# A masked attention layer and an edge-score layer in one hand-ordered kernel: two block transposes are moved to later steps, odd heads use the second score bank in the first nine slots, and the tail gets a second place for sums

## The chip, the cores and the metric

The kernel runs on one core of a Trainium2 chip. The metric is the device time of one launch in microseconds (us). Before the change it was 3078.11 us, the median of three runs (3077.22 to 3081.56).

## The reference

The input is `x`, 16 graphs of 1024 nodes with 256 features in float32, and `adj`, 16 matrices of 1024 x 1024 in int32, which hold only 0 and 1 here.

```python
# layer 0: masked attention, 8 heads of 32
h = relu(layernorm(x))
Q, K, V = (heads(h @ W.T + b) for W, b in ((Wq, bq), (Wk, bk), (Wv, bv)))
s = where(adj == 0, -inf, Q @ K.T * 32 ** -0.5)
x = x + merge_heads(softmax(s) @ V) @ Wo.T + bo
# layer 1: edge scores of one kind of edge
h = relu(layernorm(x))
e = leaky_relu((h * a_0) @ h.T, 0.2)
x = x + softmax(where(adj == 1, e, -9e15)) @ h
```

The reference has weights `a_1` to `a_3` for entries of 2 to 4 in `adj` as well. The kernel counts such entries and has a branch for them at its end, which is not entered with these inputs.

## The kernel before

**Tiles and slots.** A graph has 8 tiles of 128 rows, so there are 128 tiles in all. Tile `t` of graph `b` is worked on in slot `s = 8 b + t`. A slot has eight steps, one for each head `h` of the tile that is in work (`now`, class `Attend`). The order of all instructions is written out by hand under `tc.manual_schedule()`: each engine runs its own instructions in exactly the order in which the loop names them, and waits where its data is not there. Beside `now`, a slot carries on five other things:

- `was`, the tile of the slot before. Its heads 6 and 7 are turned in steps 0 and 1. Then come `reciprocals` (step 1, L506 and L507 on VectorE), their turn on TensorE (step 2, L515), the copy `recT` on ScalarE (step 3, L519), `combine(1)` (heads 4 to 7, step 3, L525), `combined` (L535), `output` (step 4, L540), and `residual` (step 5, L546).
- `gone`, the tile before that: its normed rows are written for layer 1 and turned.
- `edge`, a tile of layer 1 that runs `LAG` = 9 slots behind (class `Edges`): two halves of scores in steps 0 and 2, `softmax_max` in step 3 (L654), `bend`, `leak`, and the exponential in step 6. Its scores go to `sides[1]`.
- `edge_was`, layer 1's tile of the slot before: its matrix of weights `sel` is turned in step 0, gathered against the node features in steps 5 and 6 (L696), and stored (L705).
- `piece`, 128 rows of the next graph, whose queries, keys and values are projected (L267, L344).

**A head's way.** `scores(h)` (L460) makes 128 x 1024 scores on TensorE in a PSUM place of two banks. There are two such places: `sides[0]`, and `sides[1]` for heads 4 and 6 and for layer 1. `softmax_max(h)` (L472, "max(h)" below) on VectorE adds the mask, writes `p` and gives the negated row maximum `nmx`; it also frees the place. One step later `softmax_exp(h)` (L489, "exp(h)") runs on ScalarE, and two steps after the scores the head is turned so that its columns lie on the partitions. After heads 0 to 3 are turned, `combine(0)` multiplies them with the values in step 7 (L525).

**Two ways to turn.** Most heads are turned by eight TensorE transposes (L589), with copies out of PSUM (L590). Heads 0, 1, 4 and 5 (`MIXED`; only 0 and 1 in tiles with t = 7, only 4 and 5 in tiles with t = 0), and layer 1's matrix always, go "by blocks": `turn_blocks` transposes blocks of 32 x 32 on VectorE (L381), and `place_blocks` moves them with four DMAs of 128 KB to their place in `pT` (L386). All these DMAs are issued by SyncE (SP), in the written order with its other DMAs: the queries of the next tile (`load_queries`, L427, 512 KB, step 3), the keys of the next graph (in slots with t = 7 and t = 0), `keep` and the output. Loads of `adj` and `x` and the writes of projected queries (`qd`) and keys (`kd`) are issued by GpSimd (POOL).

**The order around the change.** In step `h` of the loop the written order is: scores(h), max(h), exp(h-1), then in step 3 `recT`, `combine(1)` and `combined`, then the turn of head h-2 (so head 1 is turned in step 3, head 2 in step 4), then the parts that belong to fixed steps, among them:

```python
if h == 0:
    ...
    if edge_was:
        edge_was.turn_blocks()
        edge_was.place_blocks()
if h == 1:
    ...
    if was:
        was.reciprocals()
```

so on VectorE layer 1's block transpose lies between max(0) and max(1), and the reciprocals lie between max(1) and max(2). On SP head 1's four placing DMAs are issued before the queries of the next tile.

**The tail.** After slot 127 and a last part-slot for what is left over, nine tiles of layer 1 follow one another without a layer 0 beside them: tile 7 of graph 14, and the eight tiles of the last graph (`last`). Iteration i scores tile i, turns and places tile i-1, stores tile i-3, and gathers tile i-2. The last graph's scores alternate between the two sides, and odd tiles take other buffers for some of their data (`tags`). All gathers go to `sums_place`, the first half of one PSUM bank, which has also taken the sums of `combine`; its other half is `brief`. The second such bank has the halves `early` and `late`.

Of the kernel before, what the change touches and what calls it, by code (L numbers as in the profile page):

```python
# [8 lines left out]
F32 = mybir.dt.float32  # L9
# [5 lines left out]
ALU = mybir.AluOpType  # L15
AX = mybir.AxisListType

P = 128
HEADS = 8
HD = 32  # L20
# [10 lines left out]
def by_blocks(t):  # L31
    return BY_BLOCKS.get(t, MIXED)
# [7 lines left out]
FLOOR = 1e28  # L40
# [7 lines left out]
def gnn_kernel(  # L48
# [18 lines left out]
    nc = tc.nc  # L67
    B, N, D = x.shape
    NT = N // P
    NC = D // P  # L70
    SCALE = HD ** (-0.5)
    HALF = 512
    NB = P // HD
    LAG = NT + 1
# [9 lines left out]
    work = ctx.enter_context(tc.tile_pool(name="work", bufs=2))  # L84
# [10 lines left out]
    sums_place, brief, early, late = (banks[i // 2][:, i % 2, :] for i in range(4))  # L95


    sides = [ps_s.tile([P, N], F32, tag=f"s{i}", name=f"s{i}") for i in range(2)]
# [293 lines left out]
    h1s, x1ds, masks = {}, {}, {}  # L392
# [22 lines left out]
    class Attend:  # L415
# [3 lines left out]
        def __init__(self, b, t):  # L419
            self.b, self.t = b, t  # L420
            self.rows = slice(t * P, (t + 1) * P)
            self.probs, self.turned = {}, {}

        def load_queries(self):
            self.qt = work.tile([P, HEADS, P], F32R, tag="qt")
# [28 lines left out]
            )  # L454

        def scores(self, h):
            self.ps = sides[h in (4, 6)]
            for nh in range(N // HALF):
                cols = slice(nh * HALF, (nh + 1) * HALF)
                nc.tensor.matmul(  # L460
                    self.ps[:, cols],
                    lhsT=self.qt[:, h, :],
                    rhs=keysets[self.b][h][:, cols],
                    start=True,
                    stop=True,
                )

        def softmax_max(self, h):

            p = work.tile([P, N], F32, tag="p", bufs=4)  # L470
            nmx = small.tile([P, 1], F32, tag="nmx")
            nc.vector.tensor_tensor_reduce(  # L472
                out=p, in0=sides[h in (4, 6)], in1=self.neg, scale=-SCALE, scalar=FLOOR,
                op0=ALU.add, op1=ALU.min, accum_out=nmx,
            )
            self.probs[h] = (p, nmx)
# [116 lines left out]
    class Edges:  # L593


        def __init__(self, b, t, last=False):
            self.b, self.t, self.last = b, t, last
            self.rows = slice(t * P, (t + 1) * P)
            self.side = sides[t % 2 if last else 1]
            self.tags = {"sel": ("p", 4), "pT1": ("pT", 7)} if last else {}  # L600
            if last and t % 2:
                self.tags |= {"ha": ("hT", 1), "x1b": ("x1", 1)}

        def buffer(self, tag, shape):
            tag, bufs = self.tags.get(tag, (tag, 1))
# [86 lines left out]
        def gather(self, half):  # L692

            for j in range(half * NT // 2, (half + 1) * NT // 2):
                for a in range(NB):
                    nc.tensor.matmul(  # L696
                        sums_place[a * HD : (a + 1) * HD, :], lhsT=self.pT[:, j, a], rhs=h1s[self.b][:, j, :],
                        start=(j == 0), stop=(j == NT - 1),
                    )

        def store(self):
            rec = small.tile([P, 1], F32, tag="rec1")
            nc.vector.reciprocal(rec, self.total)  # L703
            ot = work.tile([P, D], F32, tag="h0", bufs=1)
            nc.vector.scalar_tensor_tensor(ot, sums_place, rec, self.x1, ALU.mult, ALU.add)  # L705
            nc.sync.dma_start(out=mixed(out[self.b, self.rows, :]), in_=ot)


# [76 lines left out]
    with tc.manual_schedule():  # L785
        first = [Piece(0, 0, 4), Piece(0, 4, 4)]
        piece_was, piece_next = Piece(1, 0), piece_of(0)
        now, nxt = attend_of(0), attend_of(1)
# [48 lines left out]
        for s in range(B * NT + 1):  # L837
# [9 lines left out]
            for h in range(HEADS):  # L847
                ending, eh = (now, h - 1) if h >= 1 else (was, HEADS - 1)
                turning, th = (now, h - 2) if h >= 2 else (was, HEADS + h - 2)

                load_keys(h, 0)


                if now:
                    now.scores(h)
                if h == 0 and piece_was:
                    piece_was.halve(0)
                if s == 0 and h == 1:
                    first[1].values()
                if h == 3 and edge:  # L860
                    edge.softmax_max()
                if h == 5:
                    if was:
                        was.residual()
                    norms(was, piece_nxt)
                if h == 6 and edge_was:
                    edge_was.gather(1)
                if now:
                    now.softmax_max(h)
                if h == 6 and edge_was:  # L870
                    edge_was.store()


                if h == 1 and edge:
                    edge.keep(0)
                if h == 2 and gone:
                    gone.turned_normed()
                if ending:
                    ending.softmax_exp(eh)

                if h == 3 and was:
                    was.turned_reciprocals()
                if h == 3 and edge:
                    edge.bend()
                    edge.keep(1)


                if h == 3:
                    if was:
                        was.combine(1)  # L890
                    if piece_was:
                        piece_was.biased()
                    if was:
                        was.combined()
                if turning and th in by_blocks(turning.t):
                    turning.turn_blocks(th)
                    turning.place_blocks(th)
                elif turning:
                    turning.turn(th, 0)
                    turning.turn(th, 1)  # L900


                if h == 0:
                    if edge:
                        edge.score(0)
                    if gone:
                        gone.normed()
                    if edge_was:
                        edge_was.turn_blocks()
                        edge_was.place_blocks()  # L910
                if h == 1:
                    if gone:
                        gone.turn_normed()
                    if piece_was:
                        piece_was.project(1, 0)
                        piece_was.project(1, 1)
                    if was:
                        was.reciprocals()
                    if piece_nxt:
                        piece_nxt.load()  # L920
                if h == 2:
                    if edge:
                        edge.score(1)
                    if piece_was:
                        piece_was.values()
                    if was:
                        was.turn_reciprocals()
                        was.add_bias()
                if h == 3:
                    if nxt:  # L930
                        nxt.load_queries()
                    if edge:
                        edge.leak()
                    if edge_was:
                        edge_was.load_nodes()
                    if nxt:
                        nxt.flag()
                        nxt.mask()
                if h == 4:
                    if was:  # L940
                        was.output()
                    if piece_was:
                        piece_was.raised(1)
                        piece_was.halve(1)
                    if piece:
                        piece.normed()
                    if piece_was:
                        piece_was.write_queries()
                    if edge_nxt:
                        edge_nxt.prepare()  # L950
                    if nxt2:
                        nxt2.load()
                if h == 5:
                    if edge_was:
                        edge_was.gather(0)
                    if piece:
                        piece.turn()
                    if piece:
                        piece.turned()
                if h == 6:  # L960
                    if edge:
                        edge.softmax_exp()
                    if was:
                        was.keep()
                    if now:
                        now.load_nodes()
                    if piece:
                        piece.project(0, 0)
                        piece.project(0, 1)
                if h == 7:  # L970
                    if now:
                        now.combine(0)
                    if piece:
                        piece.raised(0)
                load_keys(h, 1)
# [87 lines left out]
```

## Time and profile before

| what | value |
|---|---|
| median of three runs | 3078.11 us |
| profiled execution | 3080.43 us |
| its span, from the first instruction to the last | 3078.1 us |
| TensorE (PE) busy | 2964.1 us, 96% |
| ScalarE (ACT) busy | 2654.2 us, 86% |
| VectorE (DVE) busy | 2514.7 us, 82% |
| GpSimd (POOL) busy | 2172.2 us, 71% |
| slot 0 starts / slot 8 / slot 9 / slot 127 | 41.99 / 216.86 / 239.32 / 2970.17 us |
| length of a slot in the middle, by t from 0 to 7 | 24.4, 23.8, 23.0, 22.7, 22.5, 22.5, 22.1, 23.8 us |
| lengths of slots 1 to 4 | 19.9, 20.1, 21.7, 20.3 us |
| lengths of slots 121 to 126 | 22.4, 21.9, 21.6, 21.6, 21.5, 21.4 us |

A slot starts where scores(0) of its tile starts on PE. A line of a timeline gives the start in us, the length in us, the engine, the line of the kernel, the operation, its output and inputs, the shapes and a count of like instructions, and in square brackets the idle time of the engine just before it with what ended it. A line of the waits gives the instruction that waited, what it waited for, the total in us, how many times, and the longest. A line of the windows gives the stretch, its length, the busy time of PE, PE's weight loads, DVE, ACT and POOL (each with a count of instructions), the granted TensorE clock as a share of full speed, the busy share of the DMA engines and GB/s. A line of DMA issues ends with KB each and the median us from issue to landing.

### The profile page before, as it was taken

Reading aid. Unit: us, or ns where it says so; the run is one execution under the profiler, and the core shown is the slowest. Engines: PE = TensorE matmul, PEld = TensorE weight load, DVE = VectorE, ACT = ScalarE, POOL = GpSimd, SP = SyncE. Lnnn points to the kernel's source line nnn. Section 1 sums busy time; section 2 is a strip of 40 time slices with the busy share of each in tenths; the row PEclk is TensorE's granted clock in tenths of the full one; section 3 lists DMA queues with packets and bytes.
Section 4 is the critical chain, followed back from the end, with each engine's and each line's share of the span. In section 5 each row is a group of like instructions: output and inputs, shape, how many; then the busy total and the mean of one; then the engine's idle time right before and its main releaser. Section 6 shows DMA issues by size and latency. Waiting matters only on the chain. (4 is left out here: it accounts for less than half of the span.)

```text
span 3078.1 us, 96258 instructions
## 1 busy us (share of the span) xinstructions
PE 2964.1 (96%) x36722; PEld 2230.7 (72%) x36722; DVE 2514.7 (82%) x4453; ACT 2654.2 (86%) x5159; POOL 2172.2 (71%) x2999
## 2 busy tenths in 40 slices
PE   7889999999999999999999999999999999999997
PEld 4667777777777777777777777777777777776664
DVE  5878888888888888888888788888888888888884
ACT  5889888899888898889889888988989888898872
POOL 3657777777777777777777777777777777776542
PEclk9999999999999999999999999999999999999999
DMA  6776777878777786777777777787777777777653
GB/s 239 217 227 201 235 236 225 253 219 245 229 224 235 227 257 212 227 251 221 247 230 232 233 231 244 221 253 223 221 248 226 248 212 234 236 227 239 191 164 100
DMA packets 597828, 695.68 MB, mean 226 GB/s; under 512 B 63280, under 2 KB 528560, under 8 KB 597360
## 3 DMA queue, kind: packets, MB, share of 16 engines
q1 hardware_dynamic: 528288, 477.29, 52.0%
q0 software_dynamic: 66960, 210.04, 20.8%
q8 instruction: 295, 4.83, 0.7%
q10 hardware_dynamic: 2112, 2.10, 0.2%
q14 instruction: 173, 1.42, 0.1%
HBM read 252.98 MB, written 134.22 MB: 126 GB/s over the span
## 5 line engine op out<-in xcount | busy, mean ns | idle before, releaser
L472 DVE CUSTOM_DVE_ANT_0 p<-s,neg 128x1024 f32<-128x1024 f32 x1024 | 1235.6, 1207 | 220.8 <-PE s L460 189.5
L489 ACT ACTIVATE p<-p,nmx 128x1024 f32<-128x1024 f32 x1024 | 1249.6, 1224 | 135.5 <-DVE nmx L472 127.1
L460 PE MATMUL s<-k,qt 128*128 128x512 f32 x2048 | 759.3, 452 | 22.2 <-DVE nmx L472 13.8
L590 ACT COPY pT<-trp 128x512 f32<-128x512 f32 x1024 | 548.7, 590 | 92.8 <-PE trp L589 92.3
L589 PE MATMUL trp<-ident,p 128*128 128x128 f32 x4608 | 603.9, 274 | 3.6 <-ACT pT L590 1.5
L589 PEld LDWEIGHTS trp<-ident,p 128*128 128x128 f32 x4608 | 531.3, 140 | 101.7 <-DVE pT L590 9.6
L381 DVE STREAM_TRANSPOSE blocks<-p 128x1024 f32<-128x1024 f32 x456 | 564.4, 1238 | 12.7 <-ACT p L678 10.6
L525 PE MATMUL acc<-pT,v 128*32 128x128 f32 x16384 | 533.3, 275 | 36.9 <-ACT recT L519 24.9
L525 PEld LDWEIGHTS acc<-pT,v 128*32 128x32 f32 x16384 | 454.3, 110 | 146.3 <-ACT recT L519 79.9
L696 PE MATMUL acc<-h,pT 128*32 128x256 f32 x8192 | 493.0, 382 | 8.0 <-DVE ot L705 7.9
L440 POOL TENSOR_SCALAR neg<-adj 128x1024 bf16<-128x1024 int32 x128 | 467.7, 3654 | 43.7 <-ACT neg L452 34.4
L460 PEld LDWEIGHTS s<-k,qt 128*128 128x128 f32 x2048 | 322.0, 190 | 116.4 <-DVE nmx L472 43.7
L696 PEld LDWEIGHTS acc<-h,pT 128*32 128x32 f32 x8192 | 241.0, 109 | 210.3 <-issue 62.4
L674 POOL TENSOR_TENSOR sel<-sel,less 128x1024 f32<-128x1024 f32 x120 | 286.6, 2388 | 69.4 <-ACT less L663 48.1
L631 PE MATMUL s<-h1T,ha 128*128 128x512 f32 (+2 forms) x744 | 272.8, 490 | 2.6 <-ACT h1T L568 0.5
L672 POOL TENSOR_SCALAR less<-top 128x1 f32<-128x1 f32 x120 | 31.8, 265 | 272.9 <-DVE top L654 272.8
L324 POOL DMA_DIRECT2D qd<-halves x240 | 177.0, 777 | 58.7 <-POOL halves L314 31.8
L489 ACT ACTIVATION_READ_ACCUMULATOR p<-p,nmx 128x1 f32 x1024 | 206.8, 202 | 0.0
L509 POOL COPY wide<-rec 128x256 f32<-128x256 f32 x128 | 53.7, 419 | 208.9 <-DVE rec L507 208.9
L330 POOL DMA_DIRECT2D kd<-halves x240 | 171.7, 764 | 35.5 <-POOL halves L314 35.4
L314 POOL TENSOR_TENSOR halves<-full,halves 128x256 fp32r<-128x256 f32 x240 | 176.4, 735 | 20.6
L631 PEld LDWEIGHTS s<-h1T,ha 128*128 128x128 f32 x744 | 126.7, 190 | 70.7 <-issue 45.0
(117 smaller groups left out, 4323.1 us busy)
## 6 DMA issues: line engine op xcount, KB each, us to landing
pT<-blocks SPq DMA_DIRECT2D x2304, 128.0 KB, 3.4
qt<-qd SPq DMA_DIRECT2D x128, 512.0 KB, 4.6
k<-kd SPq DMA_DIRECT2D x128, 512.0 KB, 7.4
adj<-in_adj POOLq DMA_DIRECT2D x127, 512.0 KB, 4.9
qd<-halves POOLq DMA_DIRECT2D x240, 256.0 KB, 2.7
kd<-halves POOLq DMA_DIRECT2D x240, 128.0 KB, 4.0
xb<-in_x POOLq DMA_DIRECT2D x128, 128.0 KB, 4.1
x1d<-x SPq DMA_DIRECT2D x128, 128.0 KB, 3.8
```

The costliest lines, as they stand in the source:

```text
L324: nc.gpsimd.dma_start(out=qds[self.b][self.first, oc].rearrange("p u w n -> p u (w n)"), in_=halves.unsqueeze(1).to_broadcast([P, 2, 2 * P]),)
L381: nc.vector.transpose(blocks.rearrange("p b j q -> p j b q"), p)
L440: nc.gpsimd.tensor_scalar(self.neg, self.adj, 0.0, MASKED, ALU.is_equal, ALU.mult)
L460: nc.tensor.matmul(self.ps[:, cols], lhsT=self.qt[:, h, :], rhs=keysets[self.b][h][:, cols], start=True, stop=True,)
L472: nc.vector.tensor_tensor_reduce(out=p, in0=sides[h in (4, 6)], in1=self.neg, scale=-SCALE, scalar=FLOOR, op0=ALU.add, op1=ALU.min, accum_ ...
L489: nc.scalar.activation(to, of, AF.Exp, bias=nmx, scale=-1.0, accum_out=self.sums[:, h : h + 1])
L525: nc.tensor.matmul(sums_place[r * HD : (r + 1) * HD, g * P : (g + 1) * P], lhsT=vs[self.b][:, j, place_of(h) : place_of(h) + HD], rhs=self ...
L589: nc.tensor.transpose(tr[:, j, :], p[:, jj * P : (jj + 1) * P], ident)
L590: copy(pT[:, half * 4 : half * 4 + 4, :], tr)
L631: nc.tensor.matmul(self.side[:, cols], lhsT=self.ha[:, c, :], rhs=h1T[:, c, cols], start=(c == 0), stop=(c == NC - 1),)
L674: nc.gpsimd.tensor_tensor(self.sel, self.sel, self.less, ALU.subtract)
L696: nc.tensor.matmul(sums_place[a * HD : (a + 1) * HD, :], lhsT=self.pT[:, j, a], rhs=h1s[self.b][:, j, :], start=(j == 0), stop=(j == NT - 1),)
```

## The change

There are three edits.

1. In the first nine slots (`b * NT + t < LAG`, when there is no layer 1 yet) the odd heads' scores go to `sides[1]`, so that scores alternate between the two places. In all other slots heads 4 and 6 use it as before.
2. Layer 1's `turn_blocks` and `place_blocks` move from step 0 to step 1, behind the reciprocals. Head 1's, for tiles with t of 1 to 7, move from step 3 to step 4, ahead of the turn of head 2. Tiles with t = 0 turn head 1 on TensorE in step 3 as before. On VectorE layer 1's transpose now lies between the reciprocals and max(2), and head 1's between max(4) and the residual instead of between `combined` and max(4). On SP the load of the next tile's queries is now issued before head 1's four placing DMAs. The orders of ScalarE's and GpSimd's instructions stay the same.
3. In the tail odd tiles of the last graph gather into `late` instead of `sums_place`, and their output is written from the buffer "xb" instead of "h0".

```diff
         def __init__(self, b, t):                      # Attend
             self.b, self.t = b, t
             self.rows = slice(t * P, (t + 1) * P)
             self.probs, self.turned = {}, {}
+            self.second = (1, 3, 5, 7) if b * NT + t < LAG else (4, 6)
...
         def scores(self, h):
-            self.ps = sides[h in (4, 6)]
+            self.ps = sides[h in self.second]
...
             nc.vector.tensor_tensor_reduce(            # softmax_max
-                out=p, in0=sides[h in (4, 6)], in1=self.neg, scale=-SCALE, scalar=FLOOR,
+                out=p, in0=sides[h in self.second], in1=self.neg, scale=-SCALE, scalar=FLOOR,
...
             if last and t % 2:                         # Edges
-                self.tags |= {"ha": ("hT", 1), "x1b": ("x1", 1)}
+                self.tags |= {"ha": ("hT", 1), "x1b": ("x1", 1), "h0": ("xb", 1)}
+            self.sums = late if last and t % 2 else sums_place
...
                     nc.tensor.matmul(                  # gather
-                        sums_place[a * HD : (a + 1) * HD, :], lhsT=self.pT[:, j, a], rhs=h1s[self.b][:, j, :],
+                        self.sums[a * HD : (a + 1) * HD, :], lhsT=self.pT[:, j, a], rhs=h1s[self.b][:, j, :],
...
-            ot = work.tile([P, D], F32, tag="h0", bufs=1)
-            nc.vector.scalar_tensor_tensor(ot, sums_place, rec, self.x1, ALU.mult, ALU.add)
+            ot = self.buffer("h0", [P, D])
+            nc.vector.scalar_tensor_tensor(ot, self.sums, rec, self.x1, ALU.mult, ALU.add)
...
+                if h == 4 and now and 1 in by_blocks(t):
+                    now.turn_blocks(1)
+                    now.place_blocks(1)
                 if turning and th in by_blocks(turning.t):
-                    turning.turn_blocks(th)
-                    turning.place_blocks(th)
+                    if h != 3:
+                        turning.turn_blocks(th)
+                        turning.place_blocks(th)
...
                 if h == 0:
...
-                    if edge_was:
-                        edge_was.turn_blocks()
-                        edge_was.place_blocks()
                 if h == 1:
...
                     if was:
                         was.reciprocals()
+                    if edge_was:
+                        edge_was.turn_blocks()
+                        edge_was.place_blocks()
```

## The prediction

> **What bounds the kernel now.** I read the page first, then windows of the middle, the waits, and timelines of a steady slot, an early one and the tail.
>
> ```profile
> PE 2964.1 (96%) x36722; PEld 2230.7 (72%) x36722; DVE 2514.7 (82%) x4453; ACT 2654.2 (86%) x5159; POOL 2172.2 (71%) x2999
> 1000.00:1500.00 500.00, 495.14 (x6220) 375.68 (x6216) 422.36 (x746) 448.16 (x881) 378.00 (x525) 1.00 0.76 233
> PE acc L525 <- ACT recT L519: 24.9, 43, 1.6
> PE acc L525 <- DMA pT<-blocks: 12.0, 15, 2.0
> ```
>
> PE is the bound: in the middle it idles 1% (495.14 of 500 busy, at full clock). So a change gains only in PE's few stalls (combine(1) behind recT or a late DMA, the first nine slots, the tail), and loses where it makes a new one. The two lines of waits are the main stalls: total us, times, longest.
>
> Steps 1 to 3 of a steady slot (slot 31, t=7; it starts at 746.40), DVE, ACT, then PE:
>
> ```profile
> 748.42 1.24 DVE L381 STREAM_TRANSPOSE blocks<-sel 128x1024 f32<-128x1024 f32 x1
> 749.58 1.19 DVE L472 CUSTOM_DVE_ANT_0 p<-s,neg 128x1024 f32<-128x1024 f32 x1
> 750.90 0.20 DVE L507 RECIPROCAL rec<-rec 128x8 f32<-128x8 f32 x1
> 751.77 1.22 DVE L472 CUSTOM_DVE_ANT_0 p<-s,neg 128x1024 f32<-128x1024 f32 x1 [0.67 <-PE s L460]
> ...
> 753.10 1.15 ACT L489 ACTIVATE p<-p,nmx 128x1024 f32<-128x1024 f32 x1 [0.41 <-DVE nmx L472]
> 754.24 0.35 ACT L519 COPY recT<-acc 128x256 f32<-128x256 f32 x1
> ...
> 754.65 2.16 PE L525 MATMUL acc<-pT,v 128*32 128x128 f32 x64 [0.25 <-ACT recT L519]
> ```
>
> A chain ends at PE: max(2) (751.77) releases exp(2), recT follows it at once on ACT, and combine(1) waited 0.25 for recT. Max(2) itself sat idle 0.67 for its scores.
>
> Slots 0 and 2, PE, and the tail:
>
> ```profile
> 45.57 0.79 PE L460 MATMUL s<-k,qt 128*128 128x512 f32 x2 [2.87 <-DVE nmx L472]
> ...
> 95.69 2.16 PE L525 MATMUL acc<-pT,v 128*32 128x128 f32 x64 [0.86 <-ACT recT L519]
> ...
> 104.14 1.16 PE L267 MATMUL acc<-hT,wkT 128*128 128x128 f32 x8 [1.64 <-ACT hTm L250]
> ...
> 105.70 1.95 PE L525 MATMUL acc<-pT,v 128*32 128x128 f32 x64
> ...
> 3057.96 3.66 PE L696 MATMUL acc<-h,pT 128*32 128x256 f32 x64 [2.07 <-DVE ot L705]
> 3063.21 3.66 PE L696 MATMUL acc<-h,pT 128*32 128x256 f32 x64 [1.59 <-DVE ot L705]
> ```
>
> Scores(1) of slot 0 waits 2.87 for max(0), on the same side. Early slots stall by 0.5 to 1.6 at a time. The tail's gathers wait for the store (L705) of the tile before, which frees their one place.
>
> **Moving layer 1's transpose to step 1.** Nothing is added: 120 transposes of 1.24 (pitch 1.16 in the rows) go from before max(1) to behind the reciprocals, in front of max(2). Max(1) then waits only for its own scores: in slot 31 they end at 749.29, so it starts about 0.27 earlier (749.31) and the reciprocals end about 750.83. The transpose then fills the 0.67 hole and ends its pitch at 751.95: max(2) is 0.18 later than 751.77. Whether PE sees it depends on t. At t=7 recT follows exp(2) without a gap and PE waits already: 14 slots x 0.18 = 2.5. At t=6 the same rows leave 0.14: 14 x 0.14 = 2.0. At t=1 to 5 recT starts 0.25 to 0.67 after exp(2) has ended (it waits for PE's L515), at t=0 ACT is behind anyway: 0. In slots 121 to 127, without pieces, slots are shorter and the hole is 0.5 (max(2) of slot 124 starts at 2910.96 after idling 0.51; by the same sum it starts at 2911.28, +0.32, and combine(1), which waited 0.51 for recT there, follows); over the seven 0.32 to 0.57, taken 0.4: 2.8. Sum +7.2; ends 0 (all absorbed by jitter) and +14 (t=1 to 5 pass a part too, 70 slots x 0.1). Layer 1's four placing DMAs are issued some 2 us later; gather(0) comes only in step 5, so nothing waits; if that cover failed, PE would stop at gather(0), at most by 2 us a slot. Edge's bend and next scores do not read what moved.
>
> **Head 1 turned in step 4 (t=1 to 7), and qt's load ahead of it on SP.** Moved: one transpose (1.24) and four placing DMAs (0.6 of SP each) per slot, past max(4) on DVE; qt's 512 KB (0.61 of SP) goes ahead. Max(4) no longer has that transpose before it, and starts earlier by up to 1; the transpose itself then lies before residual (L546), which ACT sets. In steady slots the parts land 18.5 to 19 us into the slot and combine(0), step 7, comes at 20.6: hidden, with 1.5 to 2 us of cover; at t=7 20 against 21.9. Qt has until the next slot. The third user of SP is the key load (t=7), on either side alike. 0, ends -12 (below, rival B) and +5 (the sporadic late parts, now 12.0 in 15 waits, grow by half).
>
> In the short early slots the cover is thin, and is costed with the next part.
>
> **Odd heads on the second side, slots 0 to 8.** Scores(1), (3) no longer wait for the max before; the matmuls are the same number. Slot 0: the wait of 2.87 goes, the values' projections start some 1.5 earlier, and the 3.4 us at half clock that follow that gap (row 46.10 below) come at full; but exp(0) starts only at 48.48 and exp(1) behind it at 50.6 instead of 53.20, and the chain to the next projection goes with it: gain 3.3 (64.06 to 60.8), ends 0 and 5.
>
> Slots 1 to 7: exp(2)'s idle (0.4) and combine(1)'s 0.86 shrink by 0.51 together, and in slot 2 combine(0) would come 17.66 into the slot instead of 18.26 (105.70 less 87.44). Here head 1's parts decide: by the issue rows the last is issued at 14.95, behind qt. Latency from issue to landing:
>
> ```profile
> pT<-blocks SPq DMA_DIRECT2D x2304, 128.0 KB, 3.4
> ...
> pT<-blocks SPq DMA_DIRECT2D x4, 128.0 KB, 2.6
> qt<-qd SPq DMA_DIRECT2D x1, 512.0 KB, 5.3
> qd<-halves POOLq DMA_DIRECT2D x2, 256.0 KB, 6.2
> ```
>
> The first is the page's median; the rest is the end of slot 3, 119 to 126 us. With 3.4 they land at 18.35, 0.1 after combine(0) of now: seven slots, +0.7. Ends: 2.6 (17.55, the -0.54 a slot is kept: -3.8) and 5.3, qt's row, as if the parts shared its fate (20.25, +2.0 a slot: +14). I take 3.4, the like transfer's median. Slot 8 is bound by ACT: 0. Slot 9, one side for odd heads again but still short: combine(0) at 19.96, parts 0.5 later: +0.5, ends 0 and 2.
>
> The Trainium skill, DMA: Bandwidth & Descriptors, "Issuing engines are not separate DMA queues", says that DMAs begun from different engines end on the same 16 DMA engines and interleave. By it, POOL's qd writes, issued at about the same time, would slow head 1's parts in every early slot, and the sum would be that of rival A.
>
> Clock: the rows show what a hole can cost.
>
> ```profile
> 42.70:46.10 3.40, 0.53 (x2) 0.48 (x3) 1.23 (x2) 0.20 (x1) 2.93 (x4) 1.00 0.99 312
> 46.10:49.50 3.40, 3.40 (x17) 3.34 (x17) 0.42 (x1) 1.02 (x1) 2.84 (x7) 0.50 1.09 404
> 121.20:124.60 3.40, 1.72 (x11) 1.07 (x10) 3.29 (x8) 3.40 (x8) 3.02 (x5) 1.00 0.71 178
> 124.60:128.00 3.40, 3.40 (x34) 2.67 (x36) 2.66 (x4) 2.42 (x6) 2.93 (x8) 0.50 0.98 337
> ```
>
> After 3.4 us with PE busy only half (1.72), the next 3.4 run at 0.50. A hole moved from combine(1) to combine(0) may make or save one such stretch, 3.4 x 0.5 = 1.7 us: 0, ends -1.7 and +1.7. The Trainium skill, TensorE: Matmul & The Clock Gate, "What's actually happening", puts the throttle behind an idle window of about 3.4 us. By that the half-busy windows would be free and the end +1.7 nil; the row shows that they are not.
>
> **Tail, two places.** Odd tiles gather into another bank and store from another buffer, so the gather no longer waits for the store before: the waits of 0.88, 0.69, 2.07 and 1.59 (rows of 3046 to 3063) go. But the tiles come at a pitch of 5.7 us, set by DVE and ACT (transpose, max, two leak steps, exp), which stays; only the last gather counts, and it is bound by its matrix, which lands at about 3062.2 and some 0.5 earlier now: 3061.7 against 3063.21. -1.5, ends 0 (DVE's order sets all) and -3.7 (the last two waits).
>
> **Sum.** +7.2 - 3.3 + 0.7 + 0.5 - 1.5 = +3.6, other edits 0. The profiled execution took 3080.43 (span 3078.1 and 2.3 around it), 2.3 above the runs' median of 3078.11. So 3084.0 against the profiled, 3081.7 against the median; I say 3081.5, +0.11%. Less than 0.2% (6.2 us) is about what a measurement of this kernel cannot tell from no change.
>
> **Rivals.**
> - A, slower: head 1's parts land late for combine(0) in slots 1 to 7. For it: qd's 6.2 and qt's 5.3 in the rows of slot 3, and qt is now ahead on SP. Against: the parts took 2.6 in that very stretch. At 5.3 the term is +14 instead of +0.7: 3081.7 + 13.3 = 3095; it is beyond 0.2% from (14.95 + latency - 18.26) x 7 = 3.3, a latency of 3.8, and below 5.3 lies between 3085 and 3095.
> - B, faster: with qt's load issued earlier and its traffic gone by, the later placings of heads 4 and 5 find free DMA engines, and the 12.0 us that combine(1) waited for placed parts go. For it: 512 KB now run just before head 4's parts. Against: only 15 of 128 slots wait at all, and key and adjacency loads remain. 3081.7 - 12.0 = 3069.7.
> - C, the delay of max(2) never reaches PE (scores ahead of it run earlier, recT waits elsewhere): the 7.2 fall away, 3081.7 - 7.2 = 3074.5, -0.12%.
>
> **How the numbers follow.** Forecast 0.30 (3077 to 3084); A 0.28 (3085 to 3095); B 0.25 (about 3069); C 0.17 (3072 to 3077, a quarter of it beyond -0.2% with small gains of the tail and slot 0). Faster 0.25 + 0.04 = 0.29, same 0.30 + 0.13 = 0.43, slower 0.28. The range leaves out the worst third of A and a fifth of B (0.14): 3066 to 3092; the forecast's own is 3077 to 3084.
>
> **What would show it.** Right: at t=6, 7 max(2) starts with no idle before it and combine(1) waits 0.15 more for recT; max(4) starts about a us earlier; scores(1) of slot 0 has no wait on nmx and PEclk near 46 us is 1.00; in slots 1 to 7 waits for recT give way to waits for the DMA pT<-blocks at combine(0) of a few tenths; the last gather waits for its matrix, not for ot. Wrong: combine(0) waits 1 us or more in many slots (A), the line of 12.0 shrinks to a few us (B), the line of 24.9 does not grow (C), or gather(0) waits for layer 1's placing.

## The result, and the profile after

The changed kernel took 3090.34 us (median of six runs, 3086.84 to 3091.38) against 3077.36 us before (six runs, 3074.46 to 3081.56). The ratio is 1.0046, with a 95% interval of 1.0035 to 1.0056: slower by 13 us, where 3081.5 us was forecast as likeliest and 3066 to 3092 as the range. The profiled execution took 3091.38 us (span 3089.5), 11 us more than the profiled one of before.

First the page's line of the engines, then the window of the middle, then lines of the waits (total us, times, longest) of the changed kernel:

```profile
PE 2971.5 (96%) x36722; PEld 2225.6 (72%) x36722; DVE 2534.2 (82%) x4453; ACT 2645.8 (86%) x5159; POOL 2177.1 (70%) x2999
1000.00:1500.00 500.00, 492.36 (x6184) 370.87 (x6183) 422.21 (x741) 444.57 (x877) 377.74 (x516) 1.00 0.76 229
PE acc L526 <- ACT recT L520: 39.5, 57, 1.6
PE acc L526 <- DMA pT<-blocks: 12.6, 15, 2.4
PEld s L461 <- ACT mirror L647: 17.0, 75, 0.4
```

PE runs the same 36722 matmuls and idles more. In this window of the middle 492.36 of 500 us are busy instead of 495.14; over slots 9 to 120 the idle time grew less, from 37.0 to 40.6 us, and since the ends of matmuls are modelled, a part of a wait can show as busy time. The wait of combine(1) for recT grew from 24.9 to 39.5 us. The wait of scores(4)'s weight load for the mirror copies (the last line; before it was 12.4 us in 59 waits) was not on my list; PE itself may still be at work on other matmuls meanwhile. The wait for placed parts stayed in its sum, but it sits elsewhere: 6.4 of the 12.6 us now lie in slots 1 to 8, where 0.7 did.

The same steps of slot 31 as before the change, in the timeline of the changed kernel (the slot starts at 752.42; DVE, then ACT, then PE):

```profile
755.33 1.22 DVE L473 CUSTOM_DVE_ANT_0 p<-s,neg 128x1024 f32<-128x1024 f32 x1 [0.82 <-PE s L461]
756.72 0.20 DVE L508 RECIPROCAL rec<-rec 128x8 f32<-128x8 f32 x1
756.90 1.25 DVE L381 STREAM_TRANSPOSE blocks<-sel 128x1024 f32<-128x1024 f32 x1
758.07 1.19 DVE L473 CUSTOM_DVE_ANT_0 p<-s,neg 128x1024 f32<-128x1024 f32 x1
759.36 1.15 ACT L490 ACTIVATE p<-p,nmx 128x1024 f32<-128x1024 f32 x1 [0.67 <-DVE nmx L473]
760.51 0.35 ACT L520 COPY recT<-acc 128x256 f32<-128x256 f32 x1
760.91 2.50 PE L526 MATMUL acc<-pT,v 128*32 128x128 f32 x64 [0.51 <-ACT recT L520]
```

Max(2) starts 5.65 us into the slot (758.07 less 752.42) instead of 5.37, with no idle time before it. Exp(2) waits 0.67 instead of 0.41 for it, and combine(1) 0.51 instead of 0.25 for recT: a delay of 0.26 to 0.28 passes down the whole chain.

PE in slots 0 and 2 and in the tail of the changed kernel:

```profile
44.46 0.73 PE L461 MATMUL s<-k,qt 128*128 128x512 f32 x2 [2.01 <-DMA k<-kd]
...
96.07 2.16 PE L526 MATMUL acc<-pT,v 128*32 128x128 f32 x64 [1.52 <-ACT recT L520]
...
106.09 0.41 PE L526 MATMUL acc<-pT,v 128*32 128x128 f32 x2
108.19 1.95 PE L526 MATMUL acc<-pT,v 128*32 128x128 f32 x62 [1.69 <-DMA pT<-blocks]
...
3034.16 3.66 PE L698 MATMUL acc<-h,pT 128*32 128x256 f32 x64 [1.73 <-DVE h L707]
...
3067.67 5.00 PE L698 MATMUL acc<-h,pT 128*32 128x256 f32 x64 [0.63 <-DMA pT<-blocks]
3073.14 1.01 PE L698 MATMUL acc<-h,pT 128*32 128x256 f32 x4 [0.47 <-DMA pT<-blocks]
3074.34 3.64 PE L698 MATMUL acc<-h,pT 128*32 128x256 f32 x58 [0.20 <-DMA pT<-blocks]
```

In slot 0 scores(1) no longer waits for max(0), but it waits 2.01 for the key of head 1, whose load was issued at 36.59 and landed at 44.42. In slot 2 combine(0) begins at 106.09, 17.73 into the slot as the prediction had it (17.66), issues two matmuls, and stops until 108.19 for head 1's parts. In the tail one gather still waits for a store (the line at 3034.16; before, the like wait was 1.74). The later ones no longer do, and the last two wait for their own matrix.

### The profile page after: what moved, and what is told of

The parts are those of the page before. It is cut to its first block, busy times and chain, and to the rows that moved or that the text cites. A ratio compares the mean times of both kernels' runs of the same rounds, so it can differ in the third digit from the quotient of the medians.

```text
span 3089.5 us, 96379 instructions
## 1 busy us (share of the span) xinstructions
PE 2971.5 (96%) x36722; PEld 2225.6 (72%) x36722; DVE 2534.2 (82%) x4453; ACT 2645.8 (86%) x5159; POOL 2177.1 (70%) x2999
## 5 line engine op out<-in xcount | busy, mean ns | idle before, releaser
L590 PE MATMUL trp<-ident,p 128*128 128x128 f32 x4608 | 608.8, 275 | 4.3 <-ACT pT L591 2.3
L590 PEld LDWEIGHTS trp<-ident,p 128*128 128x128 f32 x4608 | 526.0, 140 | 112.9 <-ACT pT L591 25.2
L526 PE MATMUL acc<-pT,v 128*32 128x128 f32 x16384 | 532.5, 274 | 53.0 <-ACT recT L520 39.5
L381 DVE STREAM_TRANSPOSE blocks<-p 128x1024 f32<-128x1024 f32 x456 | 565.1, 1239 | 11.7 <-ACT p L680 10.6
L461 PEld LDWEIGHTS s<-k,qt 128*128 128x128 f32 x2048 | 322.4, 190 | 106.6 <-issue 35.5
L665 ACT ACTIVATE less<-sel 128x1024 f32<-128x1024 f32 x120 | 127.4, 1062 | 63.1 <-DVE top L656 61.3
```

What stands on the lines that cost most here:

```text
L381: nc.vector.transpose(blocks.rearrange("p b j q -> p j b q"), p)
L461: nc.tensor.matmul(self.ps[:, cols], lhsT=self.qt[:, h, :], rhs=keysets[self.b][h][:, cols], start=True, stop=True,)
L526: nc.tensor.matmul(sums_place[r * HD : (r + 1) * HD, g * P : (g + 1) * P], lhsT=vs[self.b][:, j, place_of(h) : place_of(h) + HD], rhs=self ...
L590: nc.tensor.transpose(tr[:, j, :], p[:, jj * P : (jj + 1) * P], ident)
```

## Where the time is: the spans between slots

A single pair of profiles misleads in the first nine slots. In them a stretch of some 3.4 us in which PE is busy about half may be followed by one at half clock, and which stretches are hit differs from one execution to the next: the profile of before has four such stretches between 46 and 172 us, other kernels with the same code there have one to three. So the table takes all profiles of the study. Each number is the time from scores(0) of one slot to scores(0) of another, in us, from the timelines.

| kernels | slots 0 to 8 | slots 9 to 120 | slots 121 to 126 |
|---|---|---|---|
| before | 197.3 | 2600.4 | 130.5 |
| changed | 200.7 | 2606.8 | 133.4 |
| all with layer 1's transpose in step 0 | | 2595.1 to 2600.7, mean of nine 2597.9 | 130.4 to 130.6 |
| all with it in step 1 (three) | | 2603.9 to 2606.8, mean 2605.1 | 133.1 to 133.4 |
| all without edit 1 and without head 1 moved (five) | 192.0 to 197.3, mean 193.3 | | |
| edit 1 without head 1 moved (three) | 187.6 to 192.5, mean 190.7 | | |
| head 1 moved without edit 1 (one) | 206.9 | | |
| both (two) | 199.4 and 200.7 | | |
| head 1 moved without edit 1, POOL's writes deferred (one) | 199.8 | | |
| edits 1 and 3, POOL's writes deferred (one) | 195.9 | | |

## The experiments

**Each part alone.** Four kernels, each the kernel before with one of the parts.

```diff
+            self.second = (1, 3, 5, 7) if b * NT + t < LAG else (4, 6)   # second_only, with its two uses
```

> The kernel before with edit 1 alone (odd heads on the second side in the first nine slots). Theory S (the side change gains by itself and its gain was eaten by head 1's late parts): the time that combine(0) comes earlier in slots 1 to 7, 0.5 us each, is kept, so 3 to 5 us less than before, less or more by one stretch at half clock (1.7 us) that moves. Rival N (the early slots are bound elsewhere, by ACT and the DMAs, so the sides do not matter): within 1 us of before.

Measured: 3070.49 us against 3074.61 us, ratio 0.9983 (0.9973 to 0.9994), 4 us less. Theory S held.

```diff
                 if h == 0:
-                    if edge_was:
-                        edge_was.turn_blocks()
-                        edge_was.place_blocks()
                 if h == 1:
                     if was:
                         was.reciprocals()
+                    if edge_was:
+                        edge_was.turn_blocks()
+                        edge_was.place_blocks()
```

> The kernel before with layer 1's transpose and placing moved to step 1, nothing else. Theory E (max(2) becomes late, and recT, bend, the mirror copies and scores(4) with it): 8 to 11 us more than before, of it 2.5 to 3.5 in slots 121 to 127, with slots of t=6 longer by 0.3 to 0.4 and t=2 to 5 by 0.05 to 0.2. Rival H (the loss of the whole change is head 1's move and the order on SP): at most 3 us more.

Measured: 3083.98 us, ratio 1.0030 (1.0018 to 1.0043), 9.4 us more. The median lengths of its slots grew by 0.08, 0.08, 0.18, 0.06, 0.36 and 0.21 us at t = 2 to 7 (the last is within the scatter of the kernels that leave the transpose in step 0), by nothing at t = 0 and 1, and slots 121 to 126 by 2.6 together. Its waits, beside those shown:

```profile
PE acc L525 <- ACT recT L519: 36.8, 59, 1.6
PEld s L460 <- ACT mirror L645: 18.6, 83, 0.4
PE acc L525 <- DMA pT<-blocks: 1.7, 4, 0.8
PEld trp L589 <- ACT pT L590: 24.4, 85, 1.9
```

The same two waits of the weight loads in the kernel before:

```profile
PEld s L460 <- ACT mirror L645: 12.4, 59, 0.4
PEld trp L589 <- ACT pT L590: 9.3, 21, 1.9
```

Both the waits for recT and those for the mirror copies are up with this one move. Theory E held, rival H fell. The third line explains why slots 9 to 120 lost 7 us on the mean of all profiles and not the 14 that the median slots would make (0.97 for t = 2 to 7, times 14). Where combine(1) comes later anyway, a part that lands late costs less: that wait took 6.1 to 11.7 us in slots 9 to 120 of the nine kernels with the transpose in step 0 (mean 9.0), and 1.7 to 6.2 in the three with it in step 1 (mean 3.9).

Where PE falls behind differs by t. These are differences of median start times in the slot, this run less before. At t = 6 and 7 combine(1) starts 0.35 and 0.25 us later, behind recT. At t = 2, 3 and 5 PE loses nothing up to scores(5) (0.02 at most). Then the transposes ahead of gather(0) (L589) start 0.06 to 0.09 later, because the copies on ACT that free their place (L590, the fourth line) run 0.22 to 0.30 later. At t = 4 scores(4) is 0.10 late behind the mirror copy, and these transposes add 0.08. At t = 2 layer 1's max, ACT's first pass over its result (`less`), the mirror copies and the copies of L590 are all late by the same 0.22: the delay of max(2) goes on through DVE's queue to layer 1's max, and from there through ACT's queue.

```diff
+                if h == 4 and now and 1 in by_blocks(t):
+                    now.turn_blocks(1)
+                    now.place_blocks(1)
                 if turning and th in by_blocks(turning.t):
-                    turning.turn_blocks(th)
-                    turning.place_blocks(th)
+                    if h != 3:
+                        turning.turn_blocks(th)
+                        turning.place_blocks(th)
```

> The kernel before with head 1's transpose and placing moved to step 4, so that the queries' load is ahead of it on SP; nothing else. Theory E: nothing in slots 9 to 127 (within 0.03 us a slot), and 3 to 8 us more in slots 1 to 7, where head 1's parts land up to 2 us after combine(0) could start. Rival H: 8 us more or above, with the loss spread over the slots of the middle. Rival Q (the queries' load out of the way of later placings): 3 us less or below.

Measured: 3084.97 us, ratio 1.0032 (1.0021 to 1.0043), 10.4 us more, somewhat above what theory E had. But the place is its place: slots 9 to 120 took 2600.7 us, as before the change, slots 0 to 8 took 206.9 (the profiled execution is a long one, 5.6 us above the median). Rivals H and Q fell. Combine(0) of slot 2 shows it:

```profile
107.28 0.41 PE L525 MATMUL acc<-pT,v 128*32 128x128 f32 x2
108.80 1.95 PE L525 MATMUL acc<-pT,v 128*32 128x128 f32 x62 [1.11 <-DMA pT<-blocks]
```

In slots 1 to 6 the time from combine(0)'s first matmul to the next slot is above its undisturbed 1.89 us by 11.7 us in all (1.6 in the profile of before); part of that is work at half clock after the stops.

```diff
-                self.tags |= {"ha": ("hT", 1), "x1b": ("x1", 1)}
+                self.tags |= {"ha": ("hT", 1), "x1b": ("x1", 1), "h0": ("xb", 1)}
+            self.sums = late if last and t % 2 else sums_place     # and its uses in gather and store
```

> The kernel before with edit 3 alone (odd tiles of the tail gather into the other bank and store from another buffer). Theory T: 0.9 to 1.5 us less than before, all of it after slot 127, with the gathers no longer waiting for the store; the pitch of the tiles stays. Rival: 3 to 4 us less, if the waits of 0.88, 0.69, 2.07 and 1.59 all come off the path.

Measured: 3072.68 us, ratio 0.9993 (0.9983 to 1.0002), 1.9 us less by the medians, which the interval does not quite set apart from nothing. Its profile has the same 1.9: from slot 127's start to the end 106.0 us instead of 107.9. So have all profiles together: a mean of 106.6 in the six with this edit and of 108.5 in the seven without, and the two groups do not overlap. The pitch of the tiles did not stay, though: the last gathers follow one another at 5.2 to 5.3 us instead of 5.3 to 5.7, and the last one is under way 3.1 us earlier after slot 127's start (3055.75 less 2965.85, against 3063.21 less 2970.17). Then it waits inside:

```profile
3055.75 4.97 PE L697 MATMUL acc<-h,pT 128*32 128x256 f32 x62 [0.18 <-DMA pT<-blocks]
```

It takes 4.97 us instead of 3.66, since it starts before its matrix has all landed (the lines of the changed kernel's last gather name that wait), and 1.3 of the 3.1 us are lost again.

The four medians add to -4.1 + 9.4 + 10.4 - 1.9 = +13.8 us, and the whole change measured +13.0; each of the four is known to about 3 us.

**What makes head 1's parts late.** In slot 2 of the changed kernel the trace gives these issues and landings (us into the slot; the last column is from the start of the issue to the landing):

```
                          issued            landed   us
queries (SP)               9.64 to 10.23    14.39    4.8
head 1, part 1 (SP)       13.10 to 13.65    15.61    2.5
head 1, part 2            13.69 to 14.29    16.29    2.6
head 1, part 3            14.34 to 14.95    17.06    2.7
qd, first write (POOL)    14.58 to 15.32    17.88    3.3
head 1, part 4            14.99 to 15.60    19.59    4.6
qd, second write (POOL)   15.24 to 16.05    19.62    4.4
adj (POOL)                15.80 to 16.62    21.73    5.9
```

The queries have landed before head 1's parts do. Three parts land in 2.5 to 2.7 us and in time; the fourth is issued behind POOL's first write of qd, takes 4.6 us and lands with the second write, 1.9 us after combine(0) has begun (17.73). Theory D is that this crossing makes it late, theory QT that the queries do.

```diff
-                    if piece_was:                 # step 4
+                    if piece_was and s >= LAG:
                         piece_was.write_queries()
-                    if nxt2:
+                    if nxt2 and s >= LAG:
                         nxt2.load()
...
                         now.load_nodes()          # step 6
+                    if piece_was and s < LAG:
+                        piece_was.write_queries()
+                    if nxt2 and s < LAG:
+                        nxt2.load()
```

> Head 1 in step 4 as in the run with that move alone, and in slots 0 to 8 POOL's two writes of projected queries and its load of adj are written behind the load of x in step 6 instead of in step 4. Theory D (the last of head 1's four DMAs falls behind POOL's writes of qd, and that is what is late): the waits of combine(0) in slots 1 to 6, 11 us together in that run, fall below 3, head 1's parts land by 18.2 in the slot, and the time is at most 3 us above before. Rival QT (the queries' load ahead of them on SP is what makes them late): as without the deferral, 8 to 12 us above before.

Measured: 3077.24 us, ratio 1.0007 (0.9995 to 1.0019), 2 us above before instead of 10. Head 1's parts land at 17.8 to 18.1 us into slots 1, 3, 4 and 5 instead of 19.2 to 20.4, and combine(0) finds them there. Theory D held, and the parts are not late with the queries still ahead of them. The run defers adj's load together with the writes of qd, so it does not part these two; the table speaks for the writes, since adj is issued only 0.8 us behind the late part. The interval holds nothing as well as the 2 us. One stop is new, though: the deferred traffic meets the parts of heads 4 and 5, and combine(1) of slot 2 stops for those of slot 1:

```profile
97.73 3.36 PE L525 MATMUL acc<-pT,v 128*32 128x128 f32 x62 [1.18 <-DMA pT<-blocks]
```

```diff
+                if h == 3 and nxt:                # ahead of head 1's transpose, still in step 3
+                    nxt.load_queries()
                 if turning and th in by_blocks(turning.t):
...
                 if h == 3:
-                    if nxt:
-                        nxt.load_queries()
```

> The kernel before, with head 1 still transposed in step 3, but the next tile's queries are loaded ahead of head 1's four placing DMAs. Theory D: the parts are issued as early as before, ahead of the writes of qd, and land by 18; within 2 us of before, slots 1 to 7 as long as before. Rival QT: 5 us more or above, with combine(0) of slots 1 to 7 waiting for head 1's parts. Rival B of the prediction (the load out of the way spares later placings): 3 us less or below.

Measured: 3074.81 us, ratio 0.9997 (0.9987 to 1.0007). The order on SP alone does nothing: in slots 2 to 5 the parts are issued between 12.3 and 14.2 us into the slot as before, ahead of qd's writes, and in slots 1 to 6 the last lands at 16.6 to 18.2. Theory QT falls by this run and the one before. Rival B of the prediction falls with it, since later placings were spared nothing that shows in the time.

**The delay of layer 1's max.** To see how far a delay on DVE passes, the same transpose was put where it delays layer 1's max (L654) by a whole transpose and leaves max(2) alone.

```diff
                 if h == 2:
+                    if edge_was:
+                        edge_was.turn_blocks()
+                        edge_was.place_blocks()
                     if edge:
                         edge.score(1)
```

> The kernel before with layer 1's transpose and placing in step 2, behind max(2) and head 0's transpose and directly ahead of layer 1's max. Theory E says that a delay of layer 1's max passes through bend and the mirror copies to scores(4), with a slack of about 0.25 us: max(2), exp(2) and recT stay on time, but layer 1's max starts 1.16 later, and slots of t=2 to 7 lose 0.6 to 0.9 each: 50 to 80 us more than before. Rival R (only recT ahead of combine(1) matters): within 3 us of before.

Measured: 3204.89 us, ratio 1.0423 (1.0407 to 1.0439), 130 us more: theory E in kind, R fell, and the size is above what was expected.

```profile
PE s L460 <- ACT mirror L645: 99.3, 101, 1.5
PE acc L525 <- ACT recT L519: 25.0, 42, 1.6
```

The wait for recT is as before the change; a new wait of scores(4) for the mirror copies has come. Slot 44 (t = 4) shows how the delay passes. First the kernel before, where the slot starts at 1052.71 (layer 1's max on DVE, combine(1) on PE, the mirror copy on ACT, scores(4) on PE):

```profile
1060.39 1.18 DVE L654 CUSTOM_DVE_ANT_0 sel<-s,neg 128x1024 f32<-128x1024 f32 x1
1061.33 2.16 PE L525 MATMUL acc<-pT,v 128*32 128x128 f32 x64
1062.59 0.57 ACT L645 COPY mirror<-s 128x512 f32<-128x512 f32 x1
1063.42 0.73 PE L460 MATMUL s<-k,qt 128*128 128x512 f32 x2
```

Then this run, where it starts at 1083.97:

```profile
1093.00 1.23 DVE L654 CUSTOM_DVE_ANT_0 sel<-s,neg 128x1024 f32<-128x1024 f32 x1
1095.23 0.57 ACT L645 COPY mirror<-s 128x512 f32<-128x512 f32 x1
1095.85 0.73 PE L460 MATMUL s<-k,qt 128*128 128x512 f32 x2 [1.10 <-ACT mirror L645]
```

Counted from the start of the slot, layer 1's max is 1.35 us later and not 1.16 (behind the second of two transposes it starts 1.35 after that one's start, behind a single one 1.16), the mirror copy 1.38, and scores(4) 1.17. So 0.21 us is absorbed. The gap from the end of the mirror copy to scores(4) shows the same: it is 0.26 before, where PE is still at combine(1), and 0.05 where PE waits, which is what the release itself takes. The slack of about 0.25 that was expected was there, as 0.21. The median slots grew by 0.84 at t = 1 and by 1.14 to 1.54 at t = 2 to 7; the transposes ahead of gather(0) add 0.08 as above, and at t = 6 and 7 another 0.2 to 0.3 comes inside the gather, which was not followed. Of the 50 us above the expected 80, the later max (0.19), the smaller slack (0.04) and the transposes (0.08) make some 26 in 84 slots, and the slots of t = 1, for which nothing had been set, 12.

**One move undone at a time.** The changed kernel with layer 1's transpose back in step 0:

> The changed kernel with layer 1's transpose back in step 0. If the parts add: -4 (sides) -2 (tail) +10 (head 1) = 2 to 7 us above before, 8 to 10 below the changed kernel; slots 9 to 127 as long as before.

Measured: 3078.04 us, ratio 1.0011 (1.0002 to 1.0020) to before, by the two ratios about 11 us below the changed kernel. Slots 9 to 120 took 2597.2 us, as without the move. And the changed kernel with head 1 back in step 3:

> The changed kernel with head 1 back in step 3. If the parts add: -4 -2 +9 = 1 to 6 us above before; combine(0) of slots 1 to 6 without the 10 us of waits, slots 9 to 127 as long as in the changed kernel.

Measured: 3081.06 us, ratio 1.0021 (1.0012 to 1.0029), which is 6.3 us above before and just over what was expected. Slots 0 to 8 took 187.6 us, slots 9 to 120 2604.5 (its profile is of its fastest execution). Each of the moves costs what it cost alone, within the intervals.

**Without the moves.** Edits 1 and 3 alone, and the same with POOL's writes deferred as above:

> Edits 1 and 3 without the two moves. If the parts add up as measured alone (about -4 and -2): 4 to 8 us below before. If the side change helps only with head 1 moved, or the tail only with its matrix earlier: within 2 us of before.

Measured: 3070.61 us, ratio 0.9986 (0.9977 to 0.9995). This beats both kernels: the one before by 4.7 us, and the changed one, by way of the two ratios, by some 18 us.

> Edits 1 and 3, and in slots 0 to 8 the writes of qd and the load of adj behind the load of x. Theory D says that head 1's parts, now issued by 13.8 in these slots, are ahead of the writes anyway: the same as edits 1 and 3 alone within 2 us. If the DMA traffic of POOL bounds the early slots in general: 3 us or more below them.

Measured: 3075.22 us, ratio 0.9998 (0.9987 to 1.0008), 4.6 us above edits 1 and 3 alone: worse than either theory had it. The parts of head 5 now land 28 to 31 us after the start of slots 1 to 5, 1 to 3 us later than with edit 1 alone, and combine(1) of slots 2, 3 and 5 is stretched to 2.8 to 4.2 us from its 1.9. Moved out of one head's way, POOL's traffic ran into another's.

## Why the prediction was right in direction and too small

The sum said +3.6 and the change cost +13.0; the forecast's own 3077 to 3084 was missed by 6 us. That 3090.3 lies inside the range is due to rival A, over which the range was drawn, and rival A, not the forecast, describes the early slots. Point by point:

- **Layer 1's transpose, +7.2.** The sign was right and the size a little low: the table has 2605.1 - 2597.9 = 7.2 us in slots 9 to 120 and 2.7 in slots 121 to 126, together 9.9, and alone it measured 9.4. The term for the last slots (2.8 with slot 127) was right. At t = 6 and 7 the way was the one forecast, through recT to combine(1), with 0.35 and 0.25 us in place of 0.14 and 0.18. In slot 31 the delay of max(2) was 0.28, since the two small instructions of the reciprocals end 0.07 later than I had them and the transpose starts behind them. The step that failed is "t = 1 to 5: 0": at t = 2 to 5 it measured 0.40 us a round of eight slots, 5.6 in all. I looked only at recT. Layer 1's max is behind max(2) on DVE, and ACT's instructions behind it come later with it: "Edge's bend and next scores do not read what moved" is true of the data, but they stand behind it in the queue. At t = 2, 3 and 5 a slack of about 0.2 us at scores(4) hid the delay of the mirror copies, and it came through at the transposes ahead of gather(0). That the total came so near is partly luck: the medians of t = 2 to 7 make 14 us, and about 5 came back because late parts cost less (3.9 instead of 9.0), which the sum did not have.
- **Head 1's move in steady slots, 0.** Right: slots 9 to 120 took 2597.0 to 2600.7 us (mean 2598.3) in the three kernels with this move and layer 1's transpose in step 0, and 2597.7 on the mean of the six with neither.
- **Head 1's move in slots 1 to 7, +0.7, and the sides there.** This is the largest miss. Combine(0) came to 17.73 as forecast (0.53 earlier; the prediction gives 0.51, 0.54 and 0.60 for it in different places), and the parts were issued as forecast (the last at 15.0). They landed at 19.6 in slots 2 to 4, so 4.6 us after the last issue, between the 3.4 that I took and the 5.3 of rival A. The median of 2304 DMAs was the wrong row: the rows beside it, 2.6 for parts that were ahead of POOL's writes and 6.2 for the writes, were two conditions, and what had to be asked was which side of POOL's issue at 14.6 the last part would fall on. The Trainium skill's sentence that I weighed and set aside (DMA: Bandwidth & Descriptors, "Issuing engines are not separate DMA queues": DMAs from different engines interleave on the same DMA engines) fits: the fourth part landed 4.6 us after its issue, with POOL's write, and the three before it after 2.5 to 2.7. With the sides and slot 0 the first nine slots cost 6.7 us on the mean of the profiles (the two with both edits against the five with neither), where the sum had -2.6 (-3.3 + 0.7; the +0.5 is slot 9's). Rival A had the place right and the price too high. Of the two causes that it named, POOL's writes of qd stand; the queries ahead on SP fall by the two runs.
- **Slot 0, -3.3.** The wait for max(0) went, and scores(1) waited 2.01 us for head 1's key instead, which landed at 44.42. In the kernel before it landed at 44.00, 1.6 us ahead of scores(1) at 45.57, so the key alone left at most 1.6 of the 2.87 to gain. The half clock near 46 us stayed too. Scores(2) came 1.9 us earlier, and what was left of that went in a second stretch at half clock at the slot's end. The first pair of windows of the changed kernel shows it, and the second pair another in slot 1 (PE busy is the second number; the clock is the third from the end):

```profile
59.30:62.70 3.40, 1.33 (x7) 0.90 (x8) 2.54 (x5) 3.40 (x8) 2.95 (x5) 0.99 0.00 0
62.70:66.10 3.40, 3.40 (x36) 2.65 (x38) 1.56 (x4) 2.30 (x6) 3.07 (x8) 0.50 0.66 212
79.70:83.10 3.40, 1.71 (x12) 1.07 (x10) 3.17 (x9) 3.40 (x9) 2.82 (x5) 1.00 0.80 214
83.10:86.50 3.40, 3.36 (x16) 2.25 (x19) 2.48 (x4) 2.64 (x6) 2.96 (x8) 0.51 0.97 298
```

  In the changed kernel with layer 1's transpose back, whose slot 0 has the same instructions, neither stretch falls there, and the slot takes 22.9 us instead of 25.5. So a gain of 2.7 us is there in one execution and gone in another. On the mean of all profiles little is left of it: 24.9 us in the six kernels with edit 1 and 25.1 in the seven without, where the sum had 3.3.
- **Slots 1 to 8, the sides alone.** That the sides gain was right: 4.1 us alone, near the prediction's own end of -3.8 for parts that land in time, and most of slots 1 to 5 at 19.2 to 19.8 instead of 19.9 to 20.3 us where no stretch at half clock falls.
- **Tail, -1.5.** Measured -1.9; right, though not by its reason: the pitch did fall, and the matrix of the last gather took back 1.3 of the 3.1 us.
- **Rival C** (the delay never reaches PE) fell with the run of layer 1's move alone, **rival B** with the queries' run.

Left open are the extra at t = 6 and 7 in the run that delays layer 1's max, and whether adj's load has a share beside POOL's writes of qd in what makes head 1's parts late.

## What to carry to other kernels

On an engine that runs in written order, price a moved instruction by everything that stands behind it in that queue up to the next idle time, and by who waits for each of those, not by the first reader alone. Follow the delay on into the queues of the other engines: here it went from VectorE's max through ScalarE's copies to transposes on TensorE two steps later. When a DMA is issued later, do not price it with the median of its kind: list what other queues issue around its new time and ask which side of them it falls on. A gap between an instruction's end and its waiter's start is slack down to the gap that is left where the waiter does wait: here 0.26 us less 0.05.

## What the runs showed of the hardware

In the first slots PE's gaps fall so that some windows of 3.41 us (in step with the changes of the clock) have PE busy about half. Over the thirteen profiles, in the first 270 us, 22 of 33 such windows with a busy share of 0.504 to 0.512 were followed by one at a clock of 0.50; of 59 at 0.54 to 0.60 none was, and of 28 between the two bands one. One stretch more or less, each worth about 1.7 us, explains a part of what sets two executions of the same early slots apart: the kernel before, with four, took 197.3 us for slots 0 to 8, and two kernels with the same early code and one each took 192.0 and 192.1; but of the two kernels with both edits, the one with five took only 1.3 us more than the one with two. The Trainium skill's rule (TensorE: Matmul & The Clock Gate, "What's actually happening"), an idle window, is not enough to tell them apart.

Of two parts of 128 KB of head 1 in slot 2, one took 2.7 us to land, its issue started 0.24 us ahead of another queue's 256 KB write, and the next took 4.6, started 0.41 us behind that write, with a second write 0.25 us behind it.
